# A graph network with four layers on one core: the order of its operations taken from a table of due dates

## The chip, the core and the metric

The kernel runs on one core of a Trainium2 chip. A core has five engines, each with an instruction queue of its own that it works off in order: TensorE (PE; its weight loads are shown as PEld), VectorE (DVE), ScalarE (ACT), GpSimd (POOL) and SyncE (SP), which here only issues DMA transfers. They are held together by semaphores alone. The metric is the time of one execution on the device in microseconds; the median of several runs counts.

## The reference, cut to what matters

There are 64 graphs of 256 nodes with 256 features each, and one adjacency matrix of integers per graph. Four layers follow each other, each with a residual and a normalization around it: attention with eight heads and a feed-forward part, two graph attention layers, and a relational convolution of two steps.

```python
# x (64, 256, 256) float32, adj (64, 256, 256) int32
def reference(x, adj, ...):
    x = _layernorm(x + _L0_gnn_ref(x, adj, ...))   # attention, norm, feed-forward, norm
    x = _layernorm(x + _L1_gnn_ref(x, adj, ...))   # graph attention with a bias
    x = _layernorm(x + _L2_gnn_ref(x, adj, ...))   # graph attention with elu
    x = _layernorm(x + _L3_gnn_ref(x, ..., adj, adj))  # two relational convolutions
    return x

# layer 0, its core
allowed = (adj > 0) | (jnp.swapaxes(adj, 1, 2) > 0) | eye
scores = jnp.where(allowed[:, None], jnp.einsum('bhqd,bhkd->bhqk', q * scale, k), -jnp.inf)
ctx = jnp.einsum('bhqk,bhkd->bhqd', jax.nn.softmax(scores, axis=-1), v)
x = _layernorm(x + ctx @ Wo.T + bo)
x = _layernorm(x + jax.nn.relu(x @ W1.T + b1) @ W2.T + b2)
# layers 1 and 2, their core
e = jax.nn.leaky_relu(f_i[:, :, None] + f_j[:, None, :], 0.2)
out = jnp.einsum('bij,bjd->bid', softmax(where(adj > 0, e, NEG_INF)), h)
# layer 3, one of its two convolutions
out = x @ w_root + b + sum_r (masks[r]^T x / deg[r]) @ w_rel[r]
```

## The kernel before

Each graph is worked on by itself. Its 256 nodes are two tiles of 128 partitions, and every activation is a tile of 128 x 2 x 256. The program is written out in full for all 64 graphs; there is no loop on the chip.

The function `graph(g)` does not issue instructions. It records operations in a `Plan`: an engine, a cost in microseconds, what is read and written, and a closure that issues the instructions. For TensorE there is also a mode, the kind of product: `full` for products over the whole array, `row` for the attention scores (L763, four products side by side, each with 32 rows of the array), and `col` for the values of the attention and the sums of its weights (L784 and L789, four side by side, each with 32 columns). Nearly all products go through one helper, so L669 stands for many lines, and groups are best told apart by their tiles.

The operations of one graph, in their order: load and transposition of the input (L659, L662); the mask's transposition (L707); query, key and value products (tiles xT and wqkv); two scores operations (L763), each followed by four exps on ScalarE (L769) and four multiplications by the mask on VectorE (L771); the values (L784, L789) with a reciprocal (L795); the product with `wo`, and the addition that reads it from its bank (L807); a normalization (`layer_norm`, L671 to L694: VectorE, then GpSimd, then ScalarE); a transposition (L620) and eight feed-forward products (tiles T and w); the product back (tiles w and hid); two more normalizations; two graph attention layers, each with its products (tiles gw and T), a spread of one column over all partitions (L854), an exp (L864) and the sum over neighbours (tiles h and e); and two convolutions with products (tiles cw and T), a split of the result into a high and a low part (L921, L922), and gathers (L934). Between the layers an activation is transposed by way of DRAM in `bounced` (L641, L645, L648). The last five graphs (`QUICK`) do this on TensorE (L631, L620) instead.

All buffers are rings. PSUM has eight banks in one ring; one scores operation takes four of them. A tile's buffer is free once all operations that hold it are done.

`schedule()` then turns the record into an order. It plays the operations through with their costs and with fixed lags between engines: whenever an engine is free, it takes, from the operations whose inputs and buffers are ready, the one with the smallest key. The due date in the key is worked out backwards: each graph is due `PERIOD` = 46 us after the graph before it, the last five graphs closer together, and each operation is due in time for those that need it. TensorE prefers to stay in its kind of product:

```python
o.due = min([due] + [a.due - (a.engine != o.engine) * 0.2 for a in o.after]) - o.cost
o.order = o.due, i
...
key = e == "PE" and last != "full" and o.mode != last, o.order
...
if last != o.mode:
    end += self.SWITCH
```

The order that comes out is fixed in the program, for all five queues. The costs appear in no instruction. On the chip every instruction waits for its semaphores where it stands in its queue.

Of the kernel before, what the change touches and what calls it, by code (L numbers as in the profile page):

```python
# [13 lines left out]
ALU = mybir.AluOpType  # L14
# [11 lines left out]

SENT, BACK = 3.0, 4.5

# [3 lines left out]
DRAM = {"rows": 6}  # L32
SMALL = {"mv": 8, "st": 4, "rstd": 8, "r": 6, "rdeg": 4}


# [21 lines left out]
class Plan:  # L57
# [9 lines left out]
    NEXT = {"DVE": 0.1}  # L67
    SWITCH = 0.1
    PERIOD = 46.0
    LAST, SPACE = 5, 0.1  # L70

# [15 lines left out]
    def op(self, engine, cost, issue, graph, reads=(), writes=(), takes=(), mode=None, port=None, lag=None):  # L87
# [30 lines left out]
        self.ops.append(o)  # L118

    def schedule(self):  # L120
        last = max(o.graph for o in self.ops) - self.LAST
        for i, o in reversed(list(enumerate(self.ops))):
            due = (min(o.graph, last) + self.SPACE * max(0, o.graph - last)) * self.PERIOD
            o.due = min([due] + [a.due - (a.engine != o.engine) * 0.2 for a in o.after]) - o.cost
            o.order = o.due, i
        slots = {r: [None] * bufs for r, (bufs, _) in self.rings.items()}
# [4 lines left out]
        for o in self.ops:  # L131
            if not o.before:
                waiting[o.engine].append(o)
        done, now = [], 0.0
# [21 lines left out]
        while len(done) < len(self.ops):  # L156
            later = []
            for e, ops in waiting.items():
# [3 lines left out]
                best = None  # L162
                for o in ops:
                    key = e == "PE" and last != "full" and o.mode != last, o.order
                    if best is not None and key >= first:
                        continue
                    if o.ready > now:
                        later.append(o.ready)
                        continue
                    at = buffers_at(o)  # L170
                    if at is None:
                        continue
                    if o.port:
                        at = max(at, port["POOL" if e == "DVE" else "DVE"])
                    if at > now:
                        later.append(at)
                        continue
                    best, first = o, key
# [6 lines left out]
                if e == "PE":  # L185
                    if last != o.mode:
                        end += self.SWITCH
                    last = o.mode
# [11 lines left out]
                for a in o.after:  # L200
                    a.ready = max(a.ready, end + self.NEXT.get(e, 0.0) if a.engine == e and not o.moves else seen + self.TO.get(a.engine, 0.0))
                    blocked[id(a)] -= 1
                    if not blocked[id(a)]:
                        waiting[a.engine].append(a)
                        later.append(a.ready)
# [9 lines left out]
def tile_gnn_stack(ctx: ExitStack, tc: tile.TileContext, t: dict, out: bass.AP):  # L215
# [272 lines left out]
    def main_path(plan):  # L488
# [86 lines left out]
        def graph(g):  # L575
# [18 lines left out]
            def load(ring, view, dtype):  # L594
                xt = tok(ring, dtype)
                op("SP", 0.85, lambda: nc.sync.dma_start(xt(), view), [], [xt])
                return xt
# [5 lines left out]
            def add_later(xt, yt, reads):  # L603

                op("POOL", 0.6, lambda: nc.gpsimd.dma_start(xt(), yt(), accum_op=ALU.add), [xt, *reads], [xt], lag=3.0)

# [6 lines left out]
            def transposed(xt):  # L613
# [7 lines left out]

                pe("full", 0.44, issue, [xt], [pt], [xT])
                act(0.47, lambda: nc.scalar.copy(xT(), pt()), [pt], [xT])  # L623
# [12 lines left out]
            def bounced(xt):  # L636
# [7 lines left out]
                for a in range(4):  # L644
                    op("SP", 0.5, lambda a=a: nc.sync.dma_start(  # L645
                        rows().rearrange("(c b) q a n -> c (b q) a n", b=4)[:, :, a, :],
                        turned()[32 * a : 32 * a + 32].rearrange("c b q n -> c (b q) n")), [turned], [(rows, a)], lag=SENT)
                op("SP", 0.5, lambda: nc.sync.dma_start(xT().rearrange("p q n -> p (q n)"), rows().rearrange("p q a n -> p (q a n)")),  # L648
                   [rows], [xT], lag=BACK)
# [21 lines left out]
            def layer_norm(y):  # L671
# [21 lines left out]
                dve(0.88, stats, [y], [mv, stat])  # L693
                op("POOL", 1.6, root, [mv], [rstd], port="waits", lag=0.4)  # L694
                act(1.0, apply, [y, rstd], [y])

            def masks(adj):
# [10 lines left out]

                pe("full", 0.22, issue, [bits], [pt], [am, gm])
                dve(0.33, lambda: nc.vector.tensor_scalar(gm(), pt(), BIG, NO_EDGE, op0=ALU.mult, op1=ALU.add), [pt], [gm])  # L710
# [10 lines left out]
            def projections(xT):  # L721

                qk, v = new("qk", [P, 2 * KB, N]), tok("v")
                for half in range(2):
                    pq = new("bank", [P, KB, N])
                    for c in range(KB):
                        n = half * KB + c
                        pe("full", 0.86, lambda n=n, c=c, pq=pq: product(
                            pq()[:, c, :], lambda kb: wqkv[:, kb, n * P : (n + 1) * P], lambda kb: xT()[:, kb, :], KB),
# [10 lines left out]
                for i in range(NB):  # L740
                    pe("full", 0.86, lambda i=i: product(pv()[:, i, :], lambda kb: xT()[:, kb, i * P : (i + 1) * P],
                                                         lambda kb: wqkv[:, kb, 2 * D : 3 * D], KB), [xT, c_wqkv],
# [4 lines left out]
            def attention(xT, am):  # L747
# [6 lines left out]
                for kt in range(NB):  # L754
# [10 lines left out]

                    pe("row", 0.97, scores, [qk], s, [p[kt, r] for r in range(4)])
                    for r in range(4):
# [23 lines left out]

                pe("col", 2.62, values, [v] + both + list(p.values()), pcs, [ctxT, inv])
                for hg in range(KB):
# [7 lines left out]
            def product_plus(lhs, reads, rhs, n, add):  # L801

                y, po = tok("X"), new("bank", [P, NB, D])
                for i in range(NB):
                    pe("full", 0.43 * n, lambda i=i: product(po()[:, i, :], lambda c: lhs(c)[:, i * P : (i + 1) * P], rhs, n),
                       reads, [po], [y])
# [3 lines left out]
            def feed_forward(x1, xt):  # L810
# [6 lines left out]
                for f in range(0, NF, 2):  # L817
                    ph = new("bank", [P, 2, N])
                    for k in range(2):
                        pe("full", 0.86, lambda f=f, k=k, ph=ph: product(  # L820
                            ph()[:, k, :], lambda kb: w1[:, kb, (f + k) * P : (f + k + 1) * P],
# [12 lines left out]
            def gat(xt, layer, gm, seen, bias, finish):  # L834
# [3 lines left out]
                for i in range(NB):  # L838
                    ph = new("bank", [P, D + 2])
                    pe("full", 0.87, lambda i=i, ph=ph: product(ph(), lambda kb: xT_at(kb, i),  # L840
                                                                lambda kb: w[:, kb, :], KB), [xT, c_w], [ph], [h])
# [14 lines left out]

                pe("full", 0.22, spread, [(h, 0), (h, 1)], [pf], [e])
                for i in range(NB):
                    dve(0.40, lambda i=i: nc.vector.scalar_tensor_tensor(e()[:, i, :], pf(), h()[:, i, G_COL : G_COL + 1],
                                                                         gm()[:, i, :], op0=ALU.add, op1=ALU.min),  # L860
# [4 lines left out]
                for i in range(NB):  # L865
                    po, r = new("bank", [P, HW]), new("r", [P, 1])
                    pe("full", 0.87, lambda i=i, po=po: product(po(), lambda kt: e()[:, kt, i * P : (i + 1) * P],
                                                                lambda kt: h()[:, kt, :], NB), [e, h], [po], [z, r])
# [4 lines left out]
            def layer1(xt, gm):  # L873
                def finish(i, z, po, r):
                    dve(0.40, lambda: nc.vector.scalar_tensor_tensor(z()[:, i, :], po()[:, 0:D], r(), xt()[:, i, :],
                                                                     op0=ALU.mult, op1=ALU.add), [po, r, xt], [(z, i)])
# [6 lines left out]
            def layer2(xt, gm):  # L883
                def finish(i, z, po, r):

                    n, zi = new("n", [P, D]), lambda: z()[:, i, :]
                    act(0.36, lambda: nc.scalar.activation(n(), po()[:, 0:D], AF.Exp, scale=r()), [po, r], [n])
                    dve(0.40, lambda: nc.vector.scalar_tensor_tensor(zi(), po()[:, 0:D], r(), xt()[:, i, :], op0=ALU.mult,
                                                                     op1=ALU.add), [po, r, xt], [(z, i)])
# [19 lines left out]
            def conv(h, layer, rel, rdeg):  # L909
# [7 lines left out]
                for i in range(NB):  # L917
                    po = new("bank", [P, 2 * D])
                    pe("full", 1.72, lambda i=i, po=po: product(po(), lambda kb: hT_at(kb, i),
                                                                lambda kb: w[:, kb, :], KB), [hT, c_w], [po], [hi, lo, o])  # L920
# [7 lines left out]
                for j in range(NB):  # L928
# [7 lines left out]

                    pe("full", 0.48, gather, [rel, hi, lo], [pa])
                    if layer == 0:
# [4 lines left out]
                        dve(0.25, inverse, [pa], [(rdeg, j)])  # L943
                    dve(0.40, lambda j=j, pa=pa: nc.vector.scalar_tensor_tensor(  # L944
                        o()[:, j, :], pa()[:, 0:D], rdeg()[:, j : j + 1], o()[:, j, :], op0=ALU.mult, op1=ALU.add),
                        [pa, (rdeg, j), (o, j)], [(o, j)])

                act(0.52, lambda: nc.scalar.activation(n(), o(), AF.Exp), [o], [n])
                act(0.52, lambda: nc.scalar.activation(n(), n(), AF.Identity, bias=minus[:, 0:1]), [n], [n])
                dve(0.60, lambda: nc.vector.scalar_tensor_tensor(o(), n(), 0.0, o(), op0=ALU.min, op1=ALU.max),  # L950
# [21 lines left out]
            layer_norm(h)  # L972
            op("SP", 0.4, lambda: nc.sync.dma_start(out_graph[g], h()), [h], [])

# [266 lines left out]
```

## Time and profile before

| what | us |
|---|---|
| median of 3 runs | 2865.24 (2865.04 to 2867.83) |
| span of the profiled execution | 2864.0 |
| first product of TensorE starts at | 12.33 |
| last product of TensorE ends at | 2851.8 |
| one scores operation (16 matmuls), start to next start | 1.07 |
| addition L807, one | 0.68 |
| one exp of scores (L769) | 0.58 |
| transfers issued on SyncE's queue | 2050, of them 944 and 236 of the transposition by way of DRAM |

A line of the profile names the source line, the engine, the operation and the tiles (`out<-in`, buffer numbers left out); `xT,wqkv` in the inputs are the moving and the standing operand. A float32 product is shown as two matmuls. "Idle before" is the time in which the engine had nothing to do just ahead of that instruction, with what ended it. The durations of matmuls are modelled and overlap, so the distance from one start to the next is what counts.

### The profile page before, as it was taken

The page shows a single profiled execution, that of the slowest core. Times are in us where ns is not written, and L with a number is a line of the kernel's source. Part 1 is how long each engine was busy: PE and PEld are TensorE (multiplying, and loading weights), DVE is VectorE, ACT ScalarE, POOL GpSimd, SP SyncE. Part 2 cuts the span into 40 slices and gives each one's busy share as a digit, 9 for nine tenths or more (in the row PEclk, how much of TensorE's full clock was granted, in tenths as well). Part 3 has the DMA queues.
Part 4 walks back from the last instruction along what each step waited for, and adds up shares of the span by engine and source line. Part 5 has one row for each costly group of instructions (what it writes and reads, how often), then busy time and mean ns, then how long its engine had stood idle before and what let it go on. Part 6 is the DMA issues. An engine that isn't in the chain of part 4 may idle for free.

```text
span 2864.0 us, 50548 instructions
## 1 busy us (share of the span) xinstructions
PE 2799.7 (98%) x16262; PEld 2130.6 (74%) x16262; DVE 2479.8 (87%) x6475; ACT 1563.8 (55%) x3753; POOL 847.5 (30%) x1747
## 2 busy tenths in 40 slices
PE   8999999999999999999999999999999999999987
PEld 6777777777777777777777777777777777777864
DVE  6889888898898899988988988999889889998677
ACT  3646554555565565555555645555555546565456
POOL 3223223232332232332323222322323223232222
PEclk9999999999999999999999999999999999999999
DMA  7455454554454455544554545555445446453211
GB/s 186 79 106 107 99 102 99 101 112 98 97 114 100 97 113 100 112 95 98 116 102 90 120 91 100 111 104 107 95 98 114 98 91 122 93 105 81 48 19 46
DMA packets 808319, 284.09 MB, mean 99 GB/s; under 512 B 651088, under 2 KB 769104, under 8 KB 808048
## 3 DMA queue, kind: packets, MB, share of 16 engines
q1 hardware_dynamic: 763680, 229.77, 36.2%
q0 software_dynamic: 44368, 51.01, 12.0%
q8 instruction: 132, 2.16, 0.3%
q14 instruction: 139, 1.14, 0.1%
HBM read 152.19 MB, written 78.64 MB: 81 GB/s over the span
## 4 chain that ended last, share of the span: by engine, by line
PE 72%; DVE 13%; DMA 7%; ACT 2%; issue 2%; SPq 2%; POOL 1%; DVEq 0%; POOLq 0%; ACTq 0%
PE bank L669 59%; DMA o<-X 3%; PE bank L934 3%; PE bank L789 3%; PE bank L763 3%; DMA rows<-turned 2%; DVE p L771 2%; PE bank L784 2%; DVE st L678 1%; SPq L645 1%; DVE turned L641 1%; DVE o L944 1%; PE bank L854 1%; DVE inv L795 1%; PE bank L620 1%
## 5 line engine op out<-in xcount | busy, mean ns | idle before, releaser
L683 POOL TENSOR_SCALAR rstd<-mv 128x2 f32<-128x2 f32 x384 | 104.6, 272 | 1456.3 <-DVE mv L680 1230.3
L669 PE MATMUL bank<-T,w 128*128 128x256 f32 x2048 | 473.2, 380 | 0.6 <-ACT T L623 0.3
L690 ACT ACTIVATE X<-X,rstd 128x256 f32<-128x256 f32 x640 | 350.1, 598 | 211.8 <-POOL rstd L686 199.3
L669 PE MATMUL bank<-cw,T 128*128 128x512 f32 x1024 | 462.7, 595 | 0.6 <-ACT T L623 0.6
L669 PE MATMUL bank<-w,hid 128*128 128x256 f32 x2048 | 459.4, 380 | 0.0
L669 PEld LDWEIGHTS bank<-T,w 128*128 128x128 f32 x2048 | 381.3, 190 | 64.7 <-issue 12.4
L669 PEld LDWEIGHTS bank<-w,hid 128*128 128x128 f32 x2048 | 385.4, 190 | 58.1 <-issue 4.3
L771 DVE TENSOR_TENSOR p<-p,am 128x512 f32<-128x512 f32 x512 | 333.7, 679 | 7.5 <-ACT p L769 7.1
L769 ACT ACTIVATE p<-bank 128x512 f32<-128x512 f32 x512 | 299.0, 597 | 75.2 <-PE bank L763 75.1
L669 PEld LDWEIGHTS bank<-cw,T 128*128 128x128 f32 x1024 | 191.5, 190 | 198.9 <-issue 182.0
L684 POOL TENSOR_TENSOR rstd<-rstd,neghalf 128x2 f32<-128x2 f32 x384 | 308.6, 804 | 32.2
L824 ACT ACTIVATE hid<-bank,col_b 128x256 f32<-128x256 f32 x512 | 207.9, 472 | 101.7 <-PE bank L669 100.8
L669 PE MATMUL bank<-xT,wqkv 128*128 128x256 f32 x1024 | 249.5, 386 | 12.3 <-DVE xT L662 12.3
L669 PE MATMUL bank<-h,e 128*128 128x259 f32 x1024 | 252.2, 386 | 7.4 <-ACT e L864 5.7
L669 PE MATMUL bank<-gw,T 128*128 128x258 f32 x1024 | 249.9, 385 | 7.2 <-DMA T<-rows 2.6
L669 PEld LDWEIGHTS bank<-h,e 128*128 128x128 f32 x1024 | 192.2, 191 | 66.8 <-issue 21.6
L678 DVE BATCH_NORM_STATS2 st<-X 128x6 f32<-128x256 f32 x640 | 236.7, 411 | 1.6
L669 PEld LDWEIGHTS bank<-xT,wqkv 128*128 128x128 f32 x1024 | 188.7, 191 | 53.8 <-issue 17.7
L795 DVE RECIPROCAL inv<-bank 128x256 f32<-128x256 f32 x128 | 219.4, 1733 | 6.1 <-PE bank L789 6.1
L669 PEld LDWEIGHTS bank<-gw,T 128*128 128x128 f32 x1024 | 191.3, 191 | 43.2 <-issue 10.0
L921 ACT CAST hi<-bank 128x256 fp32r<-128x256 f32 x256 | 94.3, 369 | 166.9 <-PE bank L669 166.6
L864 ACT ACTIVATE e<-e 128x512 f32<-128x512 f32 x128 | 80.7, 631 | 169.9 <-DVE e L862 169.2
(126 smaller groups left out, 4870.5 us busy)
## 6 DMA issues: line engine op xcount, KB each, us to landing
rows<-turned SPq DMA_DIRECT2D x944, 64.0 KB, 2.3
T<-rows SPq DMA_DIRECT2D x236, 256.0 KB, 2.8
adj<-in_adj_dram SPq DMA_DIRECT2D x128, 256.0 KB, 3.1
blocks<-in_x_dram SPq DMA_DIRECT2D x512, 32.0 KB, 2.1
x<-in_x_dram SPq DMA_DIRECT2D x64, 256.0 KB, 2.8
xr<-in_x_dram SPq DMA_DIRECT2D x64, 256.0 KB, 2.7
xr<-row_ln_b POOLq DMA_DIRECT2D x64, 256.0 KB, 4.3
x<-row_bo POOLq DMA_DIRECT2D x64, 256.0 KB, 4.7
```

The source lines that it names most:

```text
L669: nc.tensor.matmul(dst, lhsT=lhs(c), rhs=rhs(c), start=(c == 0), stop=(c == n - 1))
L678: nc.vector.bn_stats(stat()[:, i, :], y()[:, i, :])
L683: nc.gpsimd.tensor_scalar(rstd()[:, 0, :], mv()[:, :, 1], 1.0, EPS, op0=ALU.mult, op1=ALU.add)
L684: nc.gpsimd.tensor_tensor(rstd()[:, 0, :], rstd()[:, 0, :], neghalf[:, 0:NB], op=ALU.pow)
L690: nc.scalar.activation(y()[:, i, :], y()[:, i, :], AF.Identity, bias=rstd()[:, 1, i : i + 1], scale=rstd()[:, 0, i : i + 1])
L763: nc.tensor.matmul(s[r]()[:, hg, :], lhsT=qk()[f, KB + hg, kt * P : (kt + 1) * P], rhs=qk()[f, hg, :], start=True, stop=True)
L769: act(0.58, lambda pr=pr, k=k, sr=s[r]: nc.scalar.activation(pr(), sr(), AF.Exp, accum_out=seen_sum[:, k : k + 1]), [s[r]], [pr])
L771: dve(0.60, lambda pr=pr, kt=kt: nc.vector.tensor_tensor(pr(), pr(), am()[:, kt, None, :].to_broadcast([P, KB, N]), op=ALU.mult), [pr, am] ...
L789: nc.tensor.matmul(pc[32 * r : 32 * r + 32, 0, :], lhsT=v()[:, kt, HD * h : HD * (h + 1)], rhs=p[kt, r]()[:, hg, :], start=(kt == 0), stop ...
L795: dve(1.62, lambda hg=hg, pc=pc: nc.vector.reciprocal(inv()[:, hg, :], pc()[:, 1, :]), [pc], [(inv, hg)])
L824: act(0.36, lambda f=f, k=k, ph=ph: nc.scalar.activation(hid()[:, f + k, :], ph()[:, k, :], AF.Relu, bias=b1[:, f + k : f + k + 1]), [ph, ...
L921: act(0.27, lambda i=i, po=po: nc.scalar.copy(hi()[:, i, 0:D], po()[:, D:]), [po], [(hi, i)])
```

## The change

The rule for the due dates goes. In its place stand two tables. `DUE` has one number for each kind of operation of a graph. Kinds are found by comparing the lists of operations (`kinds()`): graphs whose lists are equal share their kinds, and the first graph (with the setup), those that follow, and the last ones with other lists have sets of their own. `LATER` has one number for each graph. The key of an operation is the sum of the two. The entries of `LATER` are 46 us apart from the sixth graph to about the fifty-fourth, and less near the end. The preference for the kind of product that is running goes too: the weight of a change of kind in the key, `WORTH`, is 0.

The play-through gets finer. There are seven kinds of product instead of three (transposes, spread, mask's transpose and gathers are no longer `full`), with times for entering and leaving each, and many costs are set anew. A queue looks at the first 40 waiting operations in the order of their keys. The operations themselves, their instructions, the rings and their sizes stay as they are.

```diff
-SENT, BACK = 3.0, 4.5
+SENT, BACK = 3.2, 5.5
...
+WORTH = 0.0
+DUE = [
+    -103.05, -101.12, -72.29, -42.4, -30.61, -9.7, 114.48, -9.98, -67.86, -55.49, -69.71, -28.73, -119.28, -16.83, -12.86, -156.52, -136.28, 47.78, -81.83, -165.04,
...
+]
+LATER = [
+    -59.58, 30.24, 105.62, 167.7, 184, 230, 276, 322, 368, 414, 460, 506, 552, 598, 644, 690, 736, 782, 828, 874,
...
+    1840, 1886, 1932, 1978, 2024, 2070, 2116, 2162, 2208, 2254, 2300, 2346, 2392, 2438, 2487.25, 2523.37, 2564.53, 2604.14, 2667.18, 2667.19,
+    2695.52, 2715.75, 2712.58, 2702.08,
+]
...
-    SWITCH = 0.1
-    PERIOD = 46.0
-    LAST, SPACE = 5, 0.1
+    ENTER = {"full": 0.0, "row": 0.22, "col": 0.14, "one": 0.1, "turn": 0.22, "spread": 0.11, "bits": 0.01}
+    LEAVE = {None: 0.0, "row": 0.21, "col": 0.21, "one": 0.01, "turn": 0.01, "spread": 0.02, "bits": 0.07}
+    TILED = "row", "col"
+    LOOK = 40
...
+    def switch(self, last, mode):
+
+        if mode == last:
+            return 0.0
+        if mode == "full":
+            return self.ENTER[mode] + self.LEAVE[last]
+        return self.ENTER[mode] + (0.15 if last in self.TILED and mode not in self.TILED else 0.0)
+
+    def kinds(self):
+
+        by, place, n = {}, {}, 0
+        for o in self.ops:
+            by.setdefault(o.graph, []).append(o)
+        for key in sorted(by):
+            form = tuple((o.engine, o.cost, o.mode) for o in by[key])
+            if form not in place:
+                place[form], n = n, n + len(by[key])
+            for i, o in enumerate(by[key]):
+                o.kind = place[form] + i
+        return n
+
     def schedule(self):
-        last = max(o.graph for o in self.ops) - self.LAST
-        for i, o in reversed(list(enumerate(self.ops))):
-            due = (min(o.graph, last) + self.SPACE * max(0, o.graph - last)) * self.PERIOD
-            o.due = min([due] + [a.due - (a.engine != o.engine) * 0.2 for a in o.after]) - o.cost
-            o.order = o.due, i
+        n = self.kinds()
+        assert n == len(DUE), "one due date for each kind of operation"
+        for i, o in enumerate(self.ops):
+            o.order = DUE[o.kind] + LATER[o.graph], i
...
-                for o in ops:
-                    key = e == "PE" and last != "full" and o.mode != last, o.order
+                for o in ops[: self.LOOK]:
+                    key = o.order
+                    if e == "PE":
+                        gain = self.switch(last, o.mode) if last else 0.0
+                        key = o.order[0] + WORTH * (gain - self.ENTER[o.mode]), o.order[1]
...
-                    if last != o.mode:
-                        end += self.SWITCH
+                    end += self.switch(last, o.mode) if last else 0.0
...
-                op("SP", 0.85, lambda: nc.sync.dma_start(xt(), view), [], [xt])
+                op("SP", 0.48, lambda: nc.sync.dma_start(xt(), view), [], [xt])
...
-                op("POOL", 0.6, lambda: nc.gpsimd.dma_start(xt(), yt(), accum_op=ALU.add), [xt, *reads], [xt], lag=3.0)
+                op("POOL", 1.3, lambda: nc.gpsimd.dma_start(xt(), yt(), accum_op=ALU.add), [xt, *reads], [xt], lag=3.2)
...
-                pe("full", 0.44, issue, [xt], [pt], [xT])
+                pe("turn", 0.3, issue, [xt], [pt], [xT])
...
-                op("POOL", 1.6, root, [mv], [rstd], port="waits", lag=0.4)
+                op("POOL", 1.8, root, [mv], [rstd], port="waits", lag=0.15)
...
-                    pe("row", 0.97, scores, [qk], s, [p[kt, r] for r in range(4)])
+                    pe("row", 0.87, scores, [qk], s, [p[kt, r] for r in range(4)])
...
-                pe("col", 2.62, values, [v] + both + list(p.values()), pcs, [ctxT, inv])
+                pe("col", 2.58, values, [v] + both + list(p.values()), pcs, [ctxT, inv])
...
-                    pe("full", 0.48, gather, [rel, hi, lo], [pa])
+                    pe("one", 0.46, gather, [rel, hi, lo], [pa])
```

The remaining edits are of the last kind: other costs, most of them by a few per cent, and the names `bits` and `spread` for two more kinds of product. In the instruction lists of the two programs, every queue holds the same instructions in another order.

## The prediction

> **What bounds the kernel now.** I read the page's first two parts, then the busy time by stretches, then TensorE's waits, then its timeline. Part 1 and the slices of part 2 (tenths of each slice):
>
> ```profile
> PE 2799.7 (98%) x16262; PEld 2130.6 (74%) x16262; DVE 2479.8 (87%) x6475; ACT 1563.8 (55%) x3753; POOL 847.5 (30%) x1747
> ...
> PE   8999999999999999999999999999999999999987
> ...
> DVE  6889888898898899988988988999889889998677
> ```
>
> TensorE is the bound nearly everywhere, with VectorE close behind. Busy time by stretch (PE, weight load, DVE, ACT, POOL, clock, DMA share, GB/s):
>
> ```profile
> 0.00:75.00 75.00, 60.48 (x408) 48.94 (x409) 46.64 (x104) 27.11 (x71) 23.02 (x41) 0.95 0.77 186
> 75.00:2725.00 2650.00, 2627.48 (x15380) 2004.97 (x15379) 2328.51 (x6024) 1449.29 (x3523) 791.86 (x1622) 1.00 0.50 100
> 2725.00:2864.00 139.00, 111.76 (x478) 76.69 (x476) 104.63 (x348) 87.39 (x160) 32.60 (x84) 0.94 0.14 32
> ```
>
> TensorE is idle 14.5 us at the head, 22.5 in the middle, 27.2 at the end (12.2 of them after its last product, 2851.8). A busy PE is not yet an undisturbed one, so I took the start of every matmul in the trace and the usual step to the next: 0.2155 us for 256 columns, 0.2165 for 258, 0.2175 for 259, 0.429 for 512. A block in another product kind, with its way in and out and four ordinary steps taken off, costs 1.275 for one scores operation, 2.926 for the values, 0.959 for a pair of gathers, 0.445 for a float32 transpose of a tile, 0.222 for the spread, 0.281 for the mask's transpose. Summed over the program, blocks that touch at their joint price, this is 2766.6 us. The span is 2864.0, so 97.4 are lost: 20.9 before 75 us, 41 between 75 and 2725, 23 from there to the last product, 12.2 after it. Who ended the waits from 200 to 2600 us (total, times, longest):
>
> ```profile
> PE bank L669 <- ACT e L864: 4.2, 6, 1.0
> PE bank L934 <- DVE lo L922: 3.4, 6, 1.0
> PE bank L620 <- ACT X L690: 2.8, 2, 2.7
> PE bank L669 <- DMA T<-rows: 2.6, 1, 2.6
> PE bank L669 <- ACT p L769: 2.2, 2, 1.3
> ```
>
> Small waits on many producers: no transfer and no single stage is the bound; it is whether each operand is ready when its turn comes. A change of order alone can win back part of the 97 us and of the changes of kind, nothing else. From 2725 us:
>
> ```profile
> PE bank L620 <- ACT turned L631: 6.1, 5, 3.6
> PE bank L934 <- DVE lo L922: 2.9, 3, 1.2
> PE bank L669 <- ACT T L623: 2.8, 4, 1.1
> ```
>
> There TensorE waits for the short chains of the last graphs, with nothing else left to do. Scores (qk, 16 matmuls) alone, two together, and one with a wait behind it, from three places of the timeline:
>
> ```profile
> 1003.50 1.89 PE L669 MATMUL bank<-wo,ctxT 128*128 128x256 f32 x8
> 1005.32 1.15 PE L763 MATMUL bank<-qk 32*128 32x256 f32 x16
> 1006.39 2.01 PE L669 MATMUL bank<-gw,T 128*128 128x258 f32 x8
> 1008.24 1.02 PE L669 MATMUL bank<-wqkv,xT 128*128 128x256 f32 x4
> ...
> 19.55 2.01 PE L763 MATMUL bank<-qk 32*128 32x256 f32 x32
> 21.49 0.61 PE L566 MATMUL bank<-col_ln_b,w 128*128 128x1 f32 x4
> ...
> 2573.86 1.15 PE L763 MATMUL bank<-qk 32*128 32x256 f32 x16
> 2575.94 2.01 PE L669 MATMUL bank<-gw,T 128*128 128x258 f32 x8 [0.94 <-ACT p L769]
> ```
>
> Alone: 1008.24 - 1003.50 = 4.74, less eight steps of 0.2155 and eight of 0.2165, leaves 1.28. Two together take 1.94 from start to next start, one takes 1.07: the second adds 0.87. A pair therefore saves 1.275 - 0.87 = 0.405. The last line is the price of scores badly placed: the product behind them found no free bank until an exp (L769) had read one, 0.94 us.
>
> **What the Trainium skill says.** "TensorEngine Tiling (Array Packing)", Key Properties: changing the tiling mode drains TensorE. The trace agrees: the step from a 256-column product into scores is 0.309 instead of 0.216. The same page, Gotcha 1: PSUM Pressure: different row tiles write to different PSUM banks, so row tiling presses on PSUM. Here one scores operation takes four of the eight banks, and a pair all eight. "DVE: scalar operands, raw-bit mode, write accounting and state across instructions", section 5, calls VectorE's queue one in-order queue: a late operation delays all behind it. That fits the trace: VectorE itself waits 38.0 us for the high part (L921) and 58.0 for an added tile (L678), with work queued behind.
>
> **The change part by part.** No matmul, VectorE or ScalarE operation is added, removed or resized; both programs have 9067 matmuls in their lists. The costs in the plan are no instructions. What moves is the order on all five queues. I read it from the two instruction lists.
>
> *Kinds.* Before, scores stand in pairs 2 times (and once more with other kinds behind); after, 46 times. All other couplings are worth little: values followed by scores 0.2 (7 before, 0 after), mask's transpose then tile transpose about 0.05 (45 after), others under 0.06. At joint prices all special blocks cost 553.1 before and 535.8 after: -17.
>
> *Middle.* The new order is the same from graph to graph, 44 times (before: at most 7 alike). For each product I counted the TensorE work that the order puts between it and the nearest product that its operands or its bank come from, less the measured durations of the VectorE and ScalarE steps between. Between 450 and 2500 us of work, before has 123 such links with under 0.7 us to spare, spread over high/low parts, spreads, transposes and banks. After has 102, but 91 of these are two places at the pair; 11 are left elsewhere. Bounced transposes (T<-rows) keep over 6 us. So most of the 41 us should go. I leave 18: the clock's one dip (3.4 us at half speed, at 340 us), the run-in of the first ten graphs, and VectorE's queue, which would now be 38.7 us (2479.8/64) of about 43 per graph, 90%. -23; both ends: -33 (8 left) and 0.
>
> *The pair's waits.* The second scores needs the bank that the add L807 of the attention's output reads. In the trace this add starts 0.2 us after its product's last step and takes 0.68; with 0.06 to release TensorE that is 0.94. The first scores cover 0.09 + 0.87 = 0.96. Nothing is to spare, and any lateness of VectorE reaches TensorE in full. The v product behind the pair reuses the first bank that an exp has read, with 0.2 to spare. Behind it on TensorE stands everything. The trace has hardly any such pair: 0 us waited at 19.55, 0.94 behind single scores. Bounds 0 to 1.5 (both places late); I take 0.2: 46 x 0.2 = +9.
>
> *Tail.* The order before finishes all feed-forward products 135 us before the end (the last in 2725.38) and then has chains only; the new one keeps graph 61's for 80 to 88 us of work before the end. The same count of distances falls short by 20 us before (the trace lost 23) and 5 after. With queues I leave 11: -12; ends -17 and -4. The 12.2 us after the last product are the same chain of exp, norm and store: 0.
>
> *Head.* On SP's queue wqkv now stands behind eight block loads and one xr: issued at about 5.8 us instead of 0.74. It took 4.7 to land, so 10.5 to 13.5; the first product waited for the blocks until 12.33 anyway. These come some 0.5 earlier. -0.8 to +1.7, taken +1. W1 moves behind wo, x, adj and three weight pieces, still ahead of its first use near 21 us. POOL's accumulating loads and norms move with their graphs; POOL is 30% busy, and SP issues 2050 transfers at about 0.5 us, some 16 us per graph of 43: neither binds.
>
> Sum: -17 - 23 + 9 - 12 + 1 = -42 from 2864.0, so 2822 for a profiled execution. The median is 1.2 above the span: 2823.
>
> **Rivals.**
> 1. The middle's waits stay, because VectorE's and ScalarE's queues make them and not distances. For it: VectorE at 90% and a longest wait behind DVE and ACT; against it: the 112 tight links that go. 2864 - 17 + 9 - 12 + 1 + 1 = 2846.
> 2. Slower: the pair runs out of banks. Eight exps at 0.58 must empty all eight, one add stands just ahead, and the pattern repeats it 46 times. Without it the other terms give -51; past (51 + 6)/46 = 1.24 us per pair the kernel is slower. At 1.5: +18, 2883. Against it: the count has both places just in time, and 19.55 ran free.
> 3. Better than forecast: pairs free, the middle loses 8, the tail 7: 2864 - 17 - 33 - 16 + 1 = 2799.
> 4. The table does not do what it says, orders lose and win alike: 2865. The counts above speak against it.
>
> **How the numbers follow.** Forecast 0.58, rival 1 0.20, rival 2 0.08, rival 3 0.12, rival 4 0.02. Cases below 2865 hold most of the chance; the range 2797 to 2850 takes in rival 1 and most of rival 3, and leaves out rivals 2 and 4 and the far ends. Telling from no change needs about 0.2% (6 us). Faster 0.90, same 0.02, slower 0.08.
>
> **What would show it.** Kinds: scores as x32 in the timeline, start to next near 1.94. Middle: TensorE's idle time from 75 us to the tail under 12, and starts of one graph's work about 43.4 us apart. Pair: waits of L841's matmuls (scores' new line) on DVE X L885, or of the v product on ACT p L847, near 0.2 each; 1 or more makes rival 2. Tail: idle after 2700 without ACT turned L709 as the first releaser. A median above 2850 would say that queues and not distances made the waits; above 2870 that the banks did.

## The result, and the profile after

| what | before | after |
|---|---|---|
| median, us | 2866.05 (4 runs, 2865.04 to 2867.83) | 2799.98 (4 runs, 2798.13 to 2800.20) |
| ratio of the medians | | 0.9766 (95%: 0.9752 to 0.9779) |
| span of the profiled execution, us | 2864.0 | 2796.4 |

The kernel is 2.3% faster: 66 us, where 42 were forecast. The kernel after was measured on this occasion alone. When the experiments ran, the kernel before took 2869 to 2871, so they are compared by their ratio to it; 0.001 of ratio is 2.9 us.

First the page of the kernel after, busy times and slices:

```profile
PE 2762.3 (99%) x16262; PEld 2128.1 (76%) x16262; DVE 2486.5 (89%) x6475; ACT 1568.0 (56%) x3753; POOL 855.0 (31%) x1747
...
PE   7999999999999999999999999999999999999998
...
DVE  5789999898998998998989989989989889899877
```

The numbers of instructions are the same and busy times of VectorE, ScalarE and GpSimd are within 1% of those before. TensorE has lost 37 us of busy time, and at the end only the last slice is below 9, instead of two. Busy time by stretch (PE, weight load, DVE, ACT, POOL, clock, DMA share, GB/s; the last stretch is the last 136 us, where it was the last 139 before):

```profile
0.00:75.00 75.00, 56.70 (x386) 46.10 (x387) 45.26 (x101) 25.37 (x67) 21.95 (x39) 0.95 0.74 182
75.00:2660.00 2585.00, 2584.84 (x15345) 1996.31 (x15344) 2336.86 (x6037) 1450.70 (x3517) 794.40 (x1613) 1.00 0.51 102
2660.00:2796.40 136.40, 120.74 (x534) 85.71 (x532) 104.37 (x339) 91.90 (x170) 38.63 (x95) 0.96 0.18 41
```

TensorE's idle time in the middle is 0.16 us instead of 22.5, and the list of its waits there is empty. Idle time is only part of it. As for before, I summed the undisturbed steps from start to start over the program and took what is left as lost:

| us | before | after | difference | forecast |
|---|---|---|---|---|
| undisturbed products, with changes of kind | 2766.7 | 2749.1 | -17.6 | -17 |
| lost from 75 us to the tail | 40.7 | 4.2 | -36.5 | -23, and +9 for the pairs |
| lost in the tail, up to the last product | 23.1 | 8.9 | -14.2 | -12 |
| after the last product | 12.2 | 10.9 | -1.3 | 0 |
| lost up to 75 us | 21.3 | 23.2 | +1.9 | +1 |
| sum | 2864.0 | 2796.4 | -67.7 | -42 |

The rows add up to the spans but for rounding. Only one row is far off.

A part of two rows may be TensorE's clock. The profile before shows it at half speed in one short stretch of the middle and in one of the tail (PEclk is the third number from the end):

```profile
339.80:343.20 3.40, 3.40 (x10) 2.83 (x11) 2.44 (x5) 1.56 (x3) 3.11 (x5) 0.50 0.19 30
2736.00:2742.80 6.80, 4.85 (x14) 3.99 (x15) 2.80 (x10) 4.98 (x8) 1.28 (x4) 0.50 0.13 39
```

They begin just after or during waits of TensorE of 2.65 and 3.60 us. In the profile after there is no such stretch from 75 us to the last product. Half speed can have cost up to half of each, 1.7 and 3.4 us, so that much of the gain in the two rows may be the clock's. Whether the waits bring it on was not tried.

The next view is the timeline of the kernel after at one pair of scores (start, duration, engine, line, tiles, count; in brackets idle time before and its releaser):

```profile
1031.52 1.89 PE L747 MATMUL bank<-wo,ctxT 128*128 128x256 f32 x8
...
1033.34 2.01 PE L841 MATMUL bank<-qk 32*128 32x256 f32 x32
1033.44 0.69 DVE L885 TENSOR_TENSOR X<-bank,x 128x512 f32<-128x512 f32 x1
...
1034.53 0.60 ACT L847 ACTIVATE p<-bank 128x512 f32<-128x512 f32 x1 [1.31 <-PE bank L841]
...
1035.28 1.99 PE L747 MATMUL bank<-wqkv,xT 128*128 128x256 f32 x8
```

From the start of the pair to the next product is 1035.28 - 1033.34 = 1.94, the price of a pair that waits for nothing; all 46 pairs took 1.939 or 1.940. It is as tight as the count said: the addition ends at 1034.13, 0.06 more to release makes 1034.19, and the second scores start at 1033.34 + 0.87 = 1034.21.

TensorE's waits in the last 157 us (total, times, longest), and the first product:

```profile
PE bank L698 <- ACT turned L709: 2.3, 4, 1.7
PE bank L1073 <- DVE o L1022: 1.1, 1, 1.1
PE bank L1012 <- ACT hi L999: 0.5, 1, 0.5
```

```profile
14.51 3.75 PE L747 MATMUL bank<-xT,wqkv 128*128 128x256 f32 x8 [14.51 <-DMA wqkv<-in_WqkvT_dram]
```

The same wait on `turned` leads as before, with 2.3 us instead of 6.1. At the head the first product waits for `wqkv` until 14.51 instead of for the blocks until 12.33.

Last, VectorE's own waits from 460 to 2250 us, and a regular stretch of 1700 us:

```profile
DVE inv L873 <- PE bank L867: 92.8, 42, 2.4
DVE X L885 <- PE bank L747: 47.7, 42, 1.1
```

```profile
500.00:2200.00 1700.00, 1700.00 (x10048) 1314.31 (x10048) 1550.46 (x4021) 953.96 (x2312) 537.12 (x1079) 1.00 0.53 106
```

VectorE is busy 91% of this stretch (1550.46/1700), and its free time is not scattered: 2.2 us per graph ahead of the attention's reciprocal (92.8/42), and 1.1 ahead of the addition L885 that follows the feed-forward product back (47.7/42; `X<-bank,X` in the timeline). The addition of the pair, `X<-bank,x`, is the same line, but has no gap: the queue comes to it just in time. Every regular graph now takes 42.64 to 42.67 us; before, from the 21st graph to the 58th, the same distance lay between 29.3 and 52.3, 43.6 in the mean.

### The profile page after: what moved, and what is told of

Same layout as the page of the kernel before. It is cut to its first block, busy times and chain, and to the rows that moved or that the text cites. A ratio compares the mean times of both kernels' runs of the same rounds, so it can differ in the third digit from the quotient of the medians.

```text
span 2796.4 us, 50418 instructions
## 1 busy us (share of the span) xinstructions
PE 2762.3 (99%) x16262; PEld 2128.1 (76%) x16262; DVE 2486.5 (89%) x6475; ACT 1568.0 (56%) x3753; POOL 855.0 (31%) x1747
## 5 line engine op out<-in xcount | busy, mean ns | idle before, releaser
L761 POOL TENSOR_SCALAR rstd<-mv 128x2 f32<-128x2 f32 x384 | 116.4, 303 | 1359.4 <-DVE mv L758 1226.0
L902 ACT ACTIVATE hid<-bank,col_b 128x256 f32<-128x256 f32 x512 | 213.5, 468 | 106.9 <-PE bank L747 106.6
L747 PE MATMUL bank<-xT,wqkv 128*128 128x256 f32 x1024 | 238.6, 382 | 14.5 <-DMA wqkv<-in_WqkvT_dram 14.5
L747 PEld LDWEIGHTS bank<-xT,wqkv 128*128 128x128 f32 x1024 | 193.8, 191 | 44.4 <-DVE row_b L414 14.5
L965 ACT ACTIVATE n<-bank,r 128x256 f32<-128x256 f32 x128 | 60.6, 474 | 239.6 <-DVE X L970 149.2
```

The lines of the kernel that those rows point to most:

```text
L747: nc.tensor.matmul(dst, lhsT=lhs(c), rhs=rhs(c), start=(c == 0), stop=(c == n - 1))
L761: nc.gpsimd.tensor_scalar(rstd()[:, 0, :], mv()[:, :, 1], 1.0, EPS, op0=ALU.mult, op1=ALU.add)
L902: act(0.36, lambda f=f, k=k, ph=ph: nc.scalar.activation(hid()[:, f + k, :], ph()[:, k, :], AF.Relu, bias=b1[:, f + k : f + k + 1]), [ph, ...
```

## Experiments

Line numbers shift by the lines that an edit adds. "A regular graph" is the distance from the values of one graph to those of the next, 42.66 in the kernel after.

### The pairs taken apart

In 42 regular graphs the first scores are put ahead of the product with `wo` and the second ones behind the v product, so that eight and eight matmuls stand between them; the rest of the order is kept. For this the plan is played through a second time with each queue's order fixed (`queues`), so that the buffers and semaphores fit.

```diff
...
+        ahead, pair, behind = q[i - 2 : i], q[i : i + 2], q[i + 2 : i + 4]
+        if [o.mode for o in q[i - 2 : i + 4]] == ["full", "full", "row", "row", "full", "full"] and 12 <= pair[0].graph < 54:
+            q[i - 2 : i + 4] = [pair[0], *ahead, *behind, pair[1]]
...
```

> The changed kernel with its order kept on every queue, but for one thing: in the 42 regular graphs the second scores operation stands behind the v product (four products later on TensorE) instead of right behind the first. Theory A (a pair is worth 0.405 us, and what it saves is a plain term of the sum): 42 x 0.405 = +17, so about 2817; TensorE shows single scores of 16 matmuls and no new idle time. Rival (the pairs save nothing that counts, since the emptied time would have gone into waits for banks): within 4 us of the changed kernel, 2796 to 2804. If the split also costs waits for banks it is over 2825, with idle time before scores or before the v product.

Measured: 2840.59, ratio 0.9897 (0.9881 to 0.9914), 0.0131 or 37.5 us above the kernel after, and above the 2817 of theory A. The undisturbed work is 17.3 us more, 42 times 0.41, as priced. A regular graph takes 43.57, so there are 0.50 us per graph besides; they are in TensorE's steps and nowhere in its idle time. The page of this kernel, and its timeline in one graph:

```profile
PE 2798.3 (99%) x16262; PEld 2117.6 (75%) x16262; DVE 2486.9 (88%) x6475; ACT 1574.5 (55%) x3753; POOL 860.0 (30%) x1747
```

```profile
1003.12 1.15 PE L863 MATMUL bank<-qk 32*128 32x256 f32 x16
1004.19 1.99 PE L769 MATMUL bank<-wo,ctxT 128*128 128x256 f32 x8
1006.02 1.89 PE L769 MATMUL bank<-wqkv,xT 128*128 128x256 f32 x8
1007.84 1.15 PE L863 MATMUL bank<-qk 32*128 32x256 f32 x16
...
1012.48 0.39 PE L807 MATMUL bank<-ident_b,bits 128*128 128x128 bf16 x4
1012.70 0.92 PE L720 MATMUL bank<-ident,X 128*128 128x128 f32 x4
1013.45 1.02 PE L769 MATMUL bank<-cw,T 128*128 128x512 f32 x2
```

TensorE reads 99% busy and its list of waits for the stretch from 500 to 2200 us is empty. Yet the transposition of a tile takes 1013.45 - 1012.70 = 0.75 from start to start, and in the kernel after the same step takes 0.45: it waits 0.30, and the line shows it as a longer product (0.92 instead of 0.61). The weight loads of TensorE, which are listed apart, name the producer; the second line is from their list of waits (total, times, longest, 500 to 2200 us), and the kernel after has no such entry:

```profile
1011.90 1.11 ACT L790 ACTIVATE X<-X,rstd 128x256 f32<-128x256 f32 x2
1013.07 0.31 PEld L720 LDWEIGHTS bank<-ident,X 128*128 128x128 f32 x3 [0.28 <-ACT X L790]
```

```profile
PEld bank L720 <- ACT X L790: 10.9, 39, 0.3
```

ScalarE stands still until the second scores come, works off five exps (L869, from 1009.04), and only then gets to the normalization that the transposition reads. Another 0.19 us per graph are in one set of gathers: their first product with the low part starts 0.05 after VectorE has finished a low part, and in the kernel after 0.52 after it. So taking the pairs apart costs 0.41 us per graph for the pair itself and 0.50 in queues that had been in step with it.

### The addition one place later

On VectorE's queue the addition that frees the pair's bank (number 58 of its graph's operations, counted from 0) changes places with the one behind it, a multiplication of another graph's normalization, in the same regular graphs.

```diff
...
+        if place[id(q[i])] == 58 and place[id(q[i + 1])] == 90 and 12 <= q[i].graph < 54:
+            q[i], q[i + 1] = q[i + 1], q[i]
...
```

> The changed kernel with one swap on VectorE's queue in the regular graphs: the addition that reads the bank of the attention's output product comes one operation (0.6 us) later, behind a multiplication of another graph. Theory A (nothing is to spare at the pair, a late VectorE reaches TensorE in full): TensorE waits about 0.6 us before the second scores in each of 42 graphs, +25 us, about 2825. Rival (the eight banks have room, and the pair costs no waits because it is not tight): under +5 us.

Measured: 2819.40, ratio 0.9827 (0.9810 to 0.9843), 17 us above the kernel after; a regular graph takes 43.09, so 0.43 more. The timeline:

```profile
1041.41 0.66 DVE L703 TENSOR_TENSOR X<-X,row_ln_g 128x512 f32<-128x512 f32 x1
...
1041.42 2.43 PE L866 MATMUL bank<-qk 32*128 32x256 f32 x32
...
1041.99 0.68 DVE L910 TENSOR_TENSOR X<-bank,x 128x512 f32<-128x512 f32 x1
...
1043.78 0.92 PE L772 MATMUL bank<-wqkv,xT 128*128 128x256 f32 x3
```

The addition starts 0.57 after the scores instead of 0.10, and the pair takes 1043.78 - 1041.42 = 2.36 instead of 1.94. Of a delay of 0.47 TensorE pays 0.42: the pair has 0.05 to spare at most, and it costs nothing only because the order puts the addition exactly there. TensorE's list of waits from 200 to 2600 us is again empty.

### The rule with the new costs, the table with the old ones

Two kernels, each with half of the change (the diff is the first one's). One keeps the new costs and kinds in the play-through and takes the due dates and the preference for the running kind from the old rule; the other keeps the table and takes costs, lags and kinds from before.

```diff
...
-            o.order = DUE[o.kind] + LATER[o.graph], i
...
+            due = (min(o.graph, last) + 0.1 * max(0, o.graph - last)) * 46.0
+            o.due = min([due] + [a.due - (a.engine != o.engine) * 0.2 for a in o.after]) - o.cost
+            o.order = o.due, i
...
-                        key = o.order[0] + WORTH * (gain - self.ENTER[o.mode]), o.order[1]
+                        now_in, then = (m if m in self.TILED else "full" for m in (last, o.mode))
+                        key = now_in != "full" and then != now_in, o.order
...
```

> The finer play-through of the changed kernel (its costs, lags and times for changes of kind) with the rule for due dates and the preference for a running kind of the kernel before. Theory A (the gain is in the order that the table gives): most of it goes, 2850 to 2866, with waits spread over the middle and 3 pairs of scores at most. Rival B (the gain is in the measured durations, any sensible due dates would do): 2800 to 2825.

> The table of due dates with the coarse play-through of the kernel before (its costs, three kinds of product, one time for a change). Theory A: the pairs go (2 are left in the order), +17 to +19 against the changed kernel, and some waits come back: 2818 to 2845. Rival B (the durations carry the gain): 2850 or more. Rival C (due dates alone carry it, pairs and durations hardly matter): under 2808.

Measured: 2895.51, ratio 1.0090 (1.0073 to 1.0107), and 2890.59, ratio 1.0071 (1.0055 to 1.0088). Each half alone is slower than nothing at all, and both are slower than theory A expected. The second lies where its rival B put it, that the durations carry the gain; but the first has the durations and no gain either. Both lose 57 us in the middle and have none of the gain from the kinds (2768.8 and 2768.7 us of undisturbed work, with three and two pairs). TensorE's waits of the second kernel from 200 to 2600 us:

```profile
PE bank L921 <- DVE h L912: 5.9, 8, 1.4
PE bank L736 <- DMA T<-rows: 3.4, 6, 1.0
PE bank L1001 <- ACT p L836: 3.3, 3, 1.7
```

They look like those before: small, on many producers. The due dates carry no good order of their own; of the two play-throughs tried they give one only with the finer.

### One cost one per cent higher

The next kernel shows how narrow that is. One cost in the plan is raised by 1.2%, that of the attention's reciprocal. No instruction changes; the order does.

```diff
-                        dve(1.62, ...)
+                        dve(1.64, ...)
```

> The changed kernel with one cost of the play-through altered, the reciprocal of the attention's sums from 1.62 to 1.64 us; table and rest as in the change. No instruction changes, but the play-through takes other choices: 2 pairs of scores are left in the order instead of 46. Theory A (the table is a set of numbers that gives this one good order with exactly these costs, no rule that holds nearby): +19 for the pairs and 20 to 60 of waits in the middle: 2840 to 2880. Rival (dates near the right ones do; only the pairs go): 2817 to 2825.

Measured: 2867.75 (12 runs), ratio 0.9996 (0.9986 to 1.0006). The whole gain is gone. Two pairs are left in the order, the undisturbed work is 2769.4, and the middle loses 30.4. Waits from 200 to 2600 us:

```profile
PE bank L747 <- ACT p L847: 2.9, 4, 1.2
PE bank L747 <- ACT e L942: 2.0, 2, 1.6
PE bank L932 <- DVE h L923: 1.5, 1, 1.5
```

So the gain belongs to one sequence, which the table happens to reach with these costs, and not to better due dates or better costs as such.

### The tail's entries

`LATER` keeps its 46 us for the last ten graphs too.

```diff
+LATER = [v if g < 54 else 46.0 * g for g, v in enumerate(LATER)]
```

> The changed kernel with LATER at 46 us for each of the last ten graphs, as for the regular ones; DUE and all costs as in the change. Theory A (the tail's gain comes from feed-forward work kept for the end by the crowded dates of the last graphs): the middle stays without waits, and the last 150 us lose 25 to 45 us instead of 9, since the last graph now runs mostly alone: 2815 to 2835. Rival (the last graphs overlap anyway, as TensorE is always behind its dates): under 2806.

Measured: 2841.72, ratio 0.9905 (0.9888 to 0.9922), 40 us above the kernel after. Waits from 2600 us to the end, and the last stretch:

```profile
PE bank L701 <- ACT turned L712: 22.7, 8, 5.7
PE bank L750 <- ACT T L704: 2.5, 5, 0.7
```

```profile
75.00:2660.00 2585.00, 2583.59 (x15309) 1996.27 (x15308) 2339.99 (x6056) 1456.81 (x3526) 808.27 (x1619) 1.00 0.52 103
2660.00:2840.00 180.00, 139.61 (x602) 96.44 (x600) 107.52 (x334) 92.07 (x170) 38.29 (x98) 0.89 0.09 21
```

The middle stays nearly free of idle time. The tail loses 42.3 instead of 8.9. The waits for `turned`, the last graphs' short chains, make 22.7 of it; a part is the clock, which stands at 0.89 in this stretch against 0.96 in the kernel after. The crowded last entries of the table are what fills the tail.

### The first load

On SP's queue `wqkv` goes first again.

```diff
...
+    q.insert(0, q.pop(q.index(plan.ops[0])))
...
```

> The changed kernel with its order kept on every queue, but for the load of wqkv, which is issued first on SyncE's queue as before the change, ahead of the eight block loads and one xr. Theory A (the head's +2 is this one load, which the first product waits for): the first product starts at 12.3 to 12.8 instead of 14.5, and the span falls by 1.5 to 2.2, if the wait for VectorE's sums near 31 us does not take it back. Rival (the next waits of the head, for the sums of the weights and for the small weights, swallow it): under 0.5 us. A median ratio to the kernel before of about 0.9759 against 0.9766 for the changed kernel.

Measured: 2803.10, ratio 0.9770 (0.9756 to 0.9784), no gain. The first product of this kernel:

```profile
16.76 3.78 PE L766 MATMUL bank<-xT,wqkv 128*128 128x256 f32 x8 [16.76 <-DVE xT L759]
```

Now it waits for the blocks, which VectorE transposes only at 15.99. In the other experiments with `wqkv` behind the blocks the first product starts between 15.5 and 16.7, later than the 14.51 of the kernel after. Why the blocks are so late here is open: in the kernel before `wqkv` also goes first, but no `xr` stands among the blocks, and they were transposed at 11.56.

### Is VectorE's queue the next bound?

The forecast kept 18 us of loss in the middle partly for a VectorE at 90%. Three kernels add work to its queue that writes a spare tile and nothing else: three memsets of 485 ns in every graph ahead of the reciprocal, where the 2.2 us gap lies; seven of them there; and three ahead of the addition that frees the pair's bank.

```diff
...
+                    def invert(hg=hg, pc=pc):
+                        for _ in range(3 if hg == 1 else 0):
+                            nc.vector.memset(spare, 0.0)
+                        nc.vector.reciprocal(inv()[:, hg, :], pc()[:, 1, :])
...
```

> The changed kernel, its order kept on every queue, with three memsets of a spare tile (0.45 us each) added to VectorE's queue once per graph, right ahead of the reciprocal of the attention's sums, where the trace of the changed kernel has VectorE idle for 2.2 us per graph. Theory A (waits come from distances in the order; VectorE at 90% is no bound): 1.35 of the 2.2 us are filled, TensorE sees nothing, 2798 to 2808, though VectorE goes to about 93%. Rival (the first rival of the prediction: a queue that is nearly full makes waits wherever it is loaded): +20 to +85, 2820 to 2885.

> The same with seven memsets, 3.15 us per graph, which is 0.95 more than the idle time at that place. Theory A: the surplus makes VectorE late until its next idle place, 1.1 us ahead of the addition that reads the feed-forward product, and what stands between waits: +0 to +0.95 us per graph, 2800 to 2865. Rival: VectorE would need 38.9 + 3.2 = 42.1 of 42.66 us, and the kernel goes over the one before, 2870 or more.

> The three memsets of the first of these runs, but right ahead of the addition that reads the bank of the attention's output product, which the second scores of a pair wait for. Theory A: the same load costs all but the little that is spare: +1.0 to +1.35 us in each of 64 graphs, 2865 to 2890. Rival (load counts, place does not): the same time as the run with the three memsets ahead of the reciprocal.

| kernel | median | ratio to before | a regular graph | VectorE busy, 500 to 2200 us |
|---|---|---|---|---|
| after | 2799.98 | 0.9766 (0.9752 to 0.9779) | 42.66 | 91.2% |
| 3 in the gap | 2820.22 | 0.9825 (0.9803 to 0.9846) | 42.66 | 94.6% |
| 7 in the gap | 2955.51 | 1.0303 (1.0280 to 1.0326) | 44.44 | 94.2% |
| 3 ahead of the addition | 2896.05 | 1.0090 (1.0069 to 1.0112) | 44.31 | 90.9% |

Three in the gap, the regular stretch and VectorE's waits in it:

```profile
500.00:2200.00 1700.00, 1700.00 (x10050) 1314.86 (x10049) 1609.03 (x4148) 952.80 (x2303) 536.79 (x1074) 1.00 0.53 106
```

```profile
DVE X L891 <- PE bank L748: 45.0, 40, 1.1
DVE spare L876 <- DVE spare L876: 13.9, 80, 0.2
DVE inv L877 <- PE bank L868: 11.9, 34, 0.5
```

With 94.6% (1609.03/1700) VectorE still costs TensorE nothing in this stretch: a graph takes 42.66 as before, and the gap ahead of the reciprocal shrinks to 0.35 (11.9/34), filled by three memsets and the 0.17 that each of the two later ones waits for the one before. The 0.0059 of ratio that this kernel loses all the same, 17 us, lie outside this stretch, in the graphs of the run-in and of the end, whose order is irregular and whose gaps lie elsewhere. The whole time is therefore at the lower edge of what the rival expected, while the regular graphs do what theory A expected.

Seven take 7 x 0.485 + 6 x 0.17 = 4.4, which is 2.2 over the gap, and a graph takes 1.78 longer. The load came out larger than planned, and the time is the rival's. This run doesn't tell the two theories apart: VectorE's 38.9 us per graph (0.912 x 42.66) and these 4.4 make 43.3, more than the 42.66 of a graph, wherever they stand. Three ahead of the addition take 3 x 0.485 + 2 x 0.17 = 1.8, with no gap to go into, and a graph takes 1.65 longer, which is again more than expected. The timeline of that kernel at a pair, and its waits on TensorE from 500 to 2200 us:

```profile
1026.25 1.57 PE L842 MATMUL bank<-qk 32*128 32x256 f32 x22
...
1028.78 1.13 PE L842 MATMUL bank<-qk 32*128 32x256 f32 x10 [0.96 <-DVE X L890]
1029.84 1.99 PE L748 MATMUL bank<-wqkv,xT 128*128 128x256 f32 x8
```

```profile
PE bank L842 <- DVE X L890: 36.7, 38, 1.1
```

The wait for the addition stands inside the second scores, as the step-by-step count had placed it. The first and the third of these kernels have the same load on VectorE. Where it goes into the gap, a regular graph takes no longer, at 94.6%; where it stands ahead of the addition, the graph takes 1.65 longer, at 90.9%. VectorE's share does not tell the two apart; where its free time lies does.

## Why the prediction was right in direction and short in size

*Kinds, -17 forecast.* 17.6 less was measured, from 46 pairs of 1.94; taking 42 of them apart gives back 17.3 of undisturbed work. The step holds.

*Middle, -23 forecast.* This is the failed term, mis-sized: 36.5 came off. The mechanism fits: the links with nothing to spare were counted off the two orders, 123 before and 11 away from the pairs after, and with them nearly all waits go. No experiment changed such a link alone; the pairs taken apart show that waits come back where a link gets tight, 0.30 and 0.19 us per graph. But I kept 18 of the 41 us for the clock's dip, the run-in and VectorE's queue, and 4.2 are left for all three together. The dip was kept as if it belonged to the program; the profile after has none in the middle. That the queue costs nothing in the regular graphs is shown by the three memsets in the gap. I took a share of 90% as a sign of waiting, while the same count of links that I had made for TensorE would have said for VectorE that its two gaps, 3.3 us per graph, lie just ahead of operations that TensorE releases, so that VectorE is early there and not late. Even the low end of the bounds, 8 left, was too careful.

*The pairs' waits, +9 forecast.* Nothing was measured: all 46 pairs took the price of one that runs free. The count had 0.94 to cover and 0.96 of cover; I turned this margin of 0.02 into a cost of 0.2, because a queue seemed bound to be late at times. In a sequence that repeats to 0.03 us per graph nothing is late at times. That the margin is thin is shown by the addition moved one place: 0.43 per graph at once. The forecast named only the pair at 19.55, which ran free. The trace before holds two more, and both waited. The one at 40.42 took 2.84 to the next product, and this is the other:

```profile
368.46 2.05 PE L763 MATMUL bank<-qk 32*128 32x256 f32 x32
371.76 1.57 PE L669 MATMUL bank<-gw,T 128*128 128x258 f32 x6 [1.25 <-ACT p L769]
```

It took 371.76 - 368.46 = 3.30, 1.36 more than a free pair. Here the product behind the pair waited until an exp had read a bank, as in the second rival; the new order keeps that off in all 46 pairs. The Trainium skill's page "TensorEngine Tiling (Array Packing)", Gotcha 1: PSUM Pressure, is right that row tiles press on the banks, and here the pressure costs nothing as long as the order meets it. The skill's page "DVE: scalar operands, raw-bit mode, write accounting and state across instructions", section 5, calls VectorE's queue one in-order queue, and that is what the memsets ahead of the addition show: 1.8 us of them, 1.65 paid. These two terms, 13.5 and 9, make 22.5 of the 25.7 by which the sum was short.

*Tail, -12.* 14.2 came off, inside the bounds. The entries of the last ten graphs carry it, as the kernel without them shows; up to 3.4 of it may be the clock, which the forecast had not counted here. *After the last product, 0.* 1.3 came off, but in the experiments that keep the order of the end this part takes 10.9 to 12.1, so it is no clear effect. *Head, +1.* 1.9 in the profiled executions. The mechanism was half right: `wqkv` becomes the last to arrive, at 14.5, later than the 10.5 to 13.5 worked out, because it took 9.2 us to land and not the 4.7 of before; but putting it first again wins nothing.

*Rivals.* The first, that queues make the waits whatever the distances, falls for the regular graphs with the three memsets. The second, that the pair runs out of banks, did not happen, although its trigger is close: 1.65 us per graph, above its 1.24, makes the kernel slower, as the memsets ahead of the addition show (1.0090). The third, all free, is what happened: its sum is a span of 2799, and the span came to 2796.4; that it is so close is in part luck, since its middle was 3.8 too high and its tail 1.9 too low. The fourth, that the table by itself does not do it, is half true in a sense not meant: with other costs the same table gives an order that is no better than the one before, or is worse.

## What to carry to other kernels

In a program with a fixed order, ask of each product whether its operand's distance covers the chain, and of each busy engine where its free time lies; a share of 90% says neither. The order that such a table gives belongs to its exact play-through: here one cost changed by 1.2% lost all of the gain, and the table with other costs was worth less than a simple rule. So look at the table again after any edit to a cost, a lag or an operation. Where TensorE reads 99% busy, compare the starts of the same step in two traces and read the waits of its weight loads, since short waits are inside the busy time.

## What was not expected of the hardware

Waits of TensorE up to 0.30 us (and 0.42 within a pair) appear as longer products, not as idle time: the kernel with the pairs apart has 21 us of them (42 x 0.50) at 99% busy. About half of it stands in the waits of the weight loads (10.9 us). The Trainium skill's page "Perfetto Trace Analysis", Tensor Engine Instruction (MATMUL, LD_WEIGHTS), says that the end of a matmul is computed and not observed, which fits; up to what size a wait vanishes is known only from these runs. A memset of a tile waits 0.17 us on VectorE for the memset of the same tile just ahead of it. And the whole pattern repeats to 0.03 us per graph over 44 graphs, with five engines and all their transfers in it.
